# Two reorderings in a fused scan, attention and feed-forward kernel: when the third chunk's norm is issued, and when a group norm's sums follow their transposes

## The chip, the core and the metric

The kernel runs on one core of a Trainium2 chip. A core has five engines that work side by side, each through its own list of instructions: TensorE (PE in the profile, with its weight loads as PEld), VectorE (DVE), ScalarE (ACT), GpSimd (POOL), and SyncE (SP), which issues transfers here. They wait for one another by semaphores. The metric is the device time of one execution in microseconds, the median of several executions. The kernel before takes 1202.92 us (three runs from 1202.42 to 1204.29).

## What is computed

The input is `x` of shape (4, 64, 64, 96) in float32: four images (batches) of 4096 positions with 96 channels. Cut to what matters:

```python
# layer 0
g  = group_norm(x)                          # 32 groups of 3 channels, over a whole image
xn = layer_norm(g) * gamma + beta           # per position, over 96 channels
proj = xn @ W_in + b_in                     # value, gate, delta, and A, B, C (each 96 x 16)
h_t = delta * (A_t * h_{t-1}) + delta * (B_t * value)      # a scan along the 4096 positions
y_t = sigmoid(gate) * sum_s(C_t * h_t)
x  = x + y @ W_out + b_out
# layer 1
t = x as tokens
t = t + linear_attention(layer_norm(t)) @ Wff + bff         # no softmax
t = t + quantized_ffn(layer_norm(t))                        # float8 products, 96 -> 384 -> 96
```

The group norm of an image needs sums over the whole image before its first chunk can be normalised.

## The kernel before

An image is worked in 8 chunks of 512 positions; with 4 images there are 32 chunks, numbered 0 to 31. The scan has 96 x 16 states, which are 12 tiles of 128 rows for each chunk. So there are 384 tiles, and the main loop takes one **step** for each. A chunk is 12 steps; "group 14" below means the 12 steps of chunk 14, and step 168 is its first. The names of the helpers are kept in the text: `b_proj` is three matmuls on TensorE, `b_copy` the ScalarE copy out of PSUM, and so on.

```python
for s in range(min(steps), START): call(s)        # START = 6: whatever is listed for steps below 6
for s in range(START, K):
    tiles[s + 3].b_proj(); tiles[s + 3].b_copy()  # PE; ACT
    tiles[s + 1].a_proj()                         # PE
    tiles[s].c_proj()                             # PE
    tiles[s - 1].keep()                           # ACT: last column of the scan's state
    tiles[s + 2].b_mul()                          # POOL
    if tiles[s - 1].on_pool: tiles[s - 1].c_mul_pool()     # POOL, 4 of 12 tiles
    tiles[s].scan()                               # DVE
    tiles[s + 1].a_mul()                          # DVE
    if not tiles[s].on_pool: tiles[s].c_mul()     # DVE
    call(s)                                       # the other work listed for step s, in order
    if tiles[s].on_pool: tiles[s].c_copy()        # ACT
```

Buffers that matter: PSUM has 1 bank for `b_proj`, 2 for `a_proj`, 1 + 1 for `c_proj` (even and odd tiles), and 3 ("M") for everything else. `b_proj` of the next tile cannot begin before `b_copy` of this one has ended. The order of an engine's instructions is the order in which this program emits them.

The first 54 us or so, with tiles 0 to 5 and the preparation of tiles 6 to 8, come from a list of jobs ordered by hand (`planned_start`). After it, steps from 6 on are emitted by the loop above. All other work is put into `steps` by its offset from the chunk's first step:

```python
AT = {"load_x": -39, "centre": -25, "scale": -24, "stats": -22, "rstd": -22, "apply": -21,
      "transpose": -14, "affine": -13, "upper": -13, "low": -12, ...,
      "gather1": 7, ..., "state_sum": 18, "gated": 18, "project_out": 19, "residual": 19, ...,
      "apply_f": 29, "transpose_f": 30, "quant_in": 31, ..., "sums": -31}

def front(b, i, s0, f=None):          # the norms of chunk i of image b, whose first step is s0
    ...
    plan = [("centre", f.centre, nc.gpsimd), ("scale", f.scale, nc.gpsimd),   # 1 POOL op each
            ("stats", f.stats),                   # DVE: 4 bn_stats, 4 bn_aggr
            ("rstd", f.ln.rstd),                  # POOL: 4 small operations
            ("apply", f.apply), ...]              # ACT: 4 operations
    for name, fn, *args in plan:
        at(s0 + AT[name], fn, *args)
```

Chunks 0 and 1 are normed inside `planned_start`. Chunk 2 (the third) has s0 = 24, so its centre, scale, stats, rstd and apply stand at steps -1, 0, 2, 2 and 3, all below 6, and are emitted between the planned list and step 6.

The group norm of the next image is gathered while this image is worked, one chunk at a time:

```python
def sums(self, n):
    self.transpose(n, "M", "gx")                  # PE: 4 transposes into one M bank
    for k, fn in enumerate((AF.Identity, AF.Square)):          # ACT: two passes with row sums
        nc.scalar.activation(self.ps, self.ps, fn, bias=self.c if k == 0 else 0.0,
                             accum_out=self.s[:, k, n : n + 1])

when = [s0 + AT["sums"] + NT * n for n in range(NCH)]          # NT = 12, NCH = 8
if b == 1: when = [8, 15, 22, 29, 36, 43, 50, 57]
at(when[0] - 2, make)                             # first(): 4 transposes, 2 ACT operations
for n in range(NCH):
    ...
    at(when[n], call, "sums", n)
for n, name in ((1, "moments"), (2, "mean"), (4, "root"), (6, "diagonal"), (8, "spread"),
                (8, "spread_out")):
    at(when[-1] + n, call, name)                  # moments begin with a DVE sum over self.s
```

For images 2 and 3 the sums fall on step 5 of each of the groups 5 to 20; for image 1 on the listed steps of groups 0 to 4. The group norm's entries are listed after those of the chunks, so they come last within a step. The feed-forward part of layer 1 (`apply_f` writes xn, `transpose_f` turns it on TensorE) runs one image behind, from group 10 on, at steps 5 and 6 of a group.

Of the kernel before, what the change touches and what calls it, by code (L numbers as in the profile page):

```python
# [39 lines left out]
AT = {  # L40

    "load_x": -39, "centre": -25, "scale": -24, "stats": -22, "rstd": -22, "apply": -21,
    "transpose": -14, "affine": -13, "upper": -13, "low": -12, "proj_d": -9, "d_out": -9,
    "proj_u": -9, "du_out": -9, "write": -9, "read": -6, "proj_gate": -3, "gate_out": -1,

    "gather1": 7, "gather2": 11, "gather3": 14,

    "state_sum": 18, "gated": 18, "project_out": 19, "residual": 19, "stats_a": 20,
# [5 lines left out]
    "hidden2": 38, "relu2": 38, "project_f": 40, "round_out": 40, "bias_out": 40, "total": 46,  # L54
    "store": 51,

    "sums": -31,
}
ON_POOL = (0, 2, 7, 8)
XBUFS = 15  # L60
# [3 lines left out]
def conv_attn_hybrid_kernel(  # L64
# [462 lines left out]
    def at(step, fn, *args):  # L527
        steps.setdefault(step, []).append((fn, args))
# [4 lines left out]
    class GroupNorm:  # L533
# [34 lines left out]

        def sums(self, n):
            self.transpose(n, "M", "gx")  # L570
            for k, fn in enumerate((AF.Identity, AF.Square)):
                nc.scalar.activation(
                    self.ps, self.ps, fn, bias=self.c if k == 0 else 0.0,
                    accum_out=self.s[:, k, n : n + 1],
                )
# [51 lines left out]
    def group_norm(b, s0):  # L627
        q = {}

        def make():  # L630
            q["g"] = GroupNorm(b)
            q["g"].first()

        def call(name, *args):
            getattr(q["g"], name)(*args)

        when = [s0 + AT["sums"] + NT * n for n in range(NCH)]
        if b == 1:  # L640
            when = [8, 15, 22, 29, 36, 43, 50, 57]
        if b > 1:
            at(when[0] - 7, load_gx, b, 0)
        at(when[0] - 2, make)
        for n in range(NCH):
            if n:
                at(max(when[n] - 7, when[n - 1]), load_gx, b, n)
            at(when[n], call, "sums", n)
        for n, name in ((1, "moments"), (2, "mean"), (4, "root"), (6, "diagonal"), (8, "spread"),
                        (8, "spread_out")):  # L650
            at(when[-1] + n, call, name)
# [107 lines left out]
    def front(b, i, s0, f=None):  # L759
        if f is None:  # L760
            f = Front(b, i)
            plan = [
                ("centre", f.centre, nc.gpsimd), ("scale", f.scale, nc.gpsimd), ("stats", f.stats),
                ("rstd", f.ln.rstd), ("apply", f.apply), ("transpose", f.transpose),
                ("affine", f.affine), ("upper", f.upper), ("low", f.low), ("proj_d", f.proj, 2),
                ("d_out", f.d_out), ("proj_u", f.proj, 0), ("du_out", f.du_out),
                ("write", f.write), ("read", f.read),
            ]
            if (b, i) not in xt:
                plan.insert(0, ("load_x", load_x, b, i))  # L770
        else:
            plan = []
        plan += [("proj_gate", f.proj, 1), ("gate_out", f.gate_out)]
        for name, fn, *args in plan:
            at(s0 + AT[name], fn, *args)

    state = {}
    chs = {}
# [433 lines left out]
    START = 6  # L1212
# [153 lines left out]
    for b in range(B):  # L1366
        for i in range(NCH):
            g = b * NCH + i
            s0 = g * NT
            if g:  # L1370
                front(b, i, s0, second if g == 1 else None)
            for sh in range(1, NSH):
                if g < N - 1 or sh == 1:
                    at(s0 + AT[f"gather{sh}"], gather, g, sh)
            at(s0 + NT, tail, b, i)
            s = s0 + NCH * NT
            first = min(24, AT["fetch"])
            at(s + first if b == B - 1 else min(s + first, K - 4), ffn, b, i, s)
        if b + 1 < B:
            group_norm(b + 1, b * NCH * NT)  # L1380
        s = (b + 1) * NCH * NT
        at(s if s == K else s + AT["gram_add"] - NT + 1, attn_matrix, b, s)
# [82 lines left out]
```

## Time and profile before

| | before |
|---|---|
| median of 3 runs | 1202.92 us |
| span of the profiled run | 1199.1 us |
| TensorE busy | 1148.7 us, 96% (ends of matmuls are modelled) |
| VectorE busy | 1110.0 us, 93% |
| GpSimd busy | 1032.2 us, 86% |
| ScalarE busy | 817.8 us, 68% |
| mean granted TensorE clock | 0.983 |

How the views are read. The windows view gives the busy time of each engine in a stretch, with the number of instructions in brackets, then the granted TensorE clock as a share of full speed, the busy share of the transfer engines and GB/s. The timeline lists, for each run of like instructions, its start and length in us, the engine, the line of the kernel, the operation, output<-input, and in square brackets the idle time of the engine before it and who ended that idle time. The waits view adds those idle times up by pair: us in total, times, longest. Lines of importance: 269 the projections' matmuls, 805 `b_copy`, 808 `b_mul`, 817 `a_mul`, 824 `scan`, 848 `c_mul`, 834 `keep`, 667 and 670 `centre` and `scale`, 371 and 373 `stats`, 378 to 384 and 392 `rstd`, 396 every `apply` on ScalarE, 543 and 572 the transposes and passes of `sums`, 872 `state_sum`, 910 `gated`, 915 and 920 `project_out` and `residual`, 1085 `transpose_f`.

### The profile page before, as it was taken

How to read it: one execution, taken by the hardware profiler on the slowest of the kernel's cores; microseconds unless marked ns; L12 is line 12 of the kernel's file. 1: busy time of each engine (PE TensorE's matmuls, PEld its weight loads, DVE VectorE, ACT ScalarE, POOL GpSimd, SP SyncE). 2: the span in 40 equal slices, each digit the busy share in tenths (PEclk: the TensorE clock that was granted, in tenths of full speed). 3: DMA queues.
4: the chain of work that ended last, by engine and by line, in shares of the span. 5: the costliest groups of instructions: out<-in, count | busy, mean ns of one | idle time of the engine just before them, and what ended most of it. 6: DMA issues, size and time to landing. Idle time of an engine off the chain costs nothing. (4 is left out here: it accounts for less than half of the span.)

```text
span 1199.1 us, 19211 instructions
## 1 busy us (share of the span) xinstructions
PE 1148.7 (96%) x5899; PEld 876.9 (73%) x5899; DVE 1110.0 (93%) x2091; ACT 817.8 (68%) x1828; POOL 1032.2 (86%) x1178
## 2 busy tenths in 40 slices
PE   7799999999999999999999999999999999999885
PEld 6567777677777777777777777777777777777663
DVE  6789999999999999999999999999999999999865
ACT  5465666565555777777777777777777777776476
POOL 3877888888988898999998899999999999988564
PEclk8989999999999999999999999999999999999987
DMA  7566776877776766776677677677776787667221
GB/s 187 127 127 145 153 162 159 175 156 160 168 162 150 162 156 146 175 175 156 155 158 164 152 176 177 135 160 160 163 174 153 163 181 159 151 146 165 60 74 46
DMA packets 104288, 182.12 MB, mean 152 GB/s; under 512 B 42637, under 2 KB 50769, under 8 KB 104186
## 3 DMA queue, kind: packets, MB, share of 16 engines
q1 hardware_dynamic: 90060, 106.96, 37.0%
q0 software_dynamic: 13536, 73.93, 31.0%
q8 instruction: 46, 0.75, 0.3%
q14 instruction: 56, 0.46, 0.1%
q10 hardware_dynamic: 590, 0.02, 0.0%
HBM read 69.12 MB, written 24.77 MB: 78 GB/s over the span
## 5 line engine op out<-in xcount | busy, mean ns | idle before, releaser
L808 POOL TENSOR_TENSOR bu<-bu,rep 128x512 f32<-128x512 f32 x384 | 512.3, 1342 | 53.6 <-ACT state L834 38.5
L824 DVE TENSOR_TENSOR_SCAN h<-Aps,state,bu 128x512 f32<-128x512 f32 x336 | 426.0, 1268 | 0.6 <-POOL ch L857 0.5
L805 ACT ACTIVATE bu<-Bps,b_bac 128x512 f32<-128x512 f32 x384 | 262.3, 683 | 188.7 <-PE Bps L269 185.9
L817 DVE SCALAR_TENSOR_TENSOR Aps<-Aps,b_bac,rep 128x512 f32<-128x512 f32 x384 | 281.8, 734 | 12.6 <-PE Aps L269 12.6
L269 PE MATMUL Bps<-xs,w 128*128 128x512 f32 x768 | 268.5, 431 | 16.1 <-ACT bu L805 15.6
L269 PE MATMUL Aps<-xs,w 128*128 128x512 f32 x768 | 242.4, 396 | 1.2 <-DVE h L824 1.1
L857 POOL TENSOR_TENSOR ch<-ch,h 128x512 f32<-128x512 f32 x128 | 172.5, 1348 | 14.1 <-ACT ch L854 10.7
L269 PEld LDWEIGHTS Aps<-xs,w 128*128 128x128 f32 x768 | 143.6, 188 | 38.0 <-DVE h L824 3.7
L269 PEld LDWEIGHTS Bps<-xs,w 128*128 128x128 f32 x768 | 126.5, 191 | 61.1 <-ACT bu L805 26.3
L269 PE MATMUL Aps<-xl,w 128*128 128x512 f32 x384 | 151.9, 396 | 0.0
L269 PE MATMUL Bps<-xl,w 128*128 128x512 f32 x384 | 151.8, 395 | 0.0
L269 PE MATMUL Dps<-xs,w 128*128 128x512 f32 x384 | 121.0, 396 | 0.0
L269 PE MATMUL Cps<-xs,w 128*128 128x512 f32 x384 | 120.7, 395 | 0.3 <-ACT ch L854 0.3
L848 DVE SCALAR_TENSOR_TENSOR ch<-Dps,b_bac,h 128x512 f32<-128x512 f32 x160 | 118.6, 741 | 0.8 <-PE Dps L269 0.7
L863 POOL DMA_DIRECT2D ch<-ch x94 | 90.1, 958 | 0.8 <-DMA ch<-ch 0.8
L269 PEld LDWEIGHTS Bps<-xl,w 128*128 128x128 f32 x384 | 72.5, 189 | 17.7
L269 PEld LDWEIGHTS Dps<-xs,w 128*128 128x128 f32 x384 | 72.3, 188 | 17.6
L269 PEld LDWEIGHTS Aps<-xl,w 128*128 128x128 f32 x384 | 72.2, 188 | 17.7
L269 PEld LDWEIGHTS Cps<-xs,w 128*128 128x128 f32 x384 | 71.9, 188 | 17.9 <-ACT ch L854 0.4
L854 ACT ACTIVATE ch<-Cps,b_bac 128x512 f32<-128x512 f32 x96 | 65.8, 685 | 22.9 <-PE Cps L269 22.9
L269 PE MATMUL Dps<-xl,w 128*128 128x512 f32 x192 | 75.8, 395 | 0.0
L269 PE MATMUL Cps<-xl,w 128*128 128x512 f32 x192 | 75.7, 394 | 0.0
(200 smaller groups left out, 2048.2 us busy)
## 6 DMA issues: line engine op xcount, KB each, us to landing
ch<-ch POOLq DMA_DIRECT2D x94, 768.0 KB, 6.6
rep<-ddd SPq DMA_DIRECT2D x124, 384.0 KB, 7.0
ddd<-dd SPq DMA_DIRECT2D x31, 384.0 KB, 3.2
xl<-lo SPq DMA_DIRECT2D x62, 128.0 KB, 2.5
x<-in_x_dram SPq DMA_DIRECT2D x32, 192.0 KB, 2.9
xatd<-xat SPq DMA_DIRECT2D x32, 192.0 KB, 3.6
xal<-xatd SPq DMA_DIRECT2D x32, 192.0 KB, 2.9
out_dram<-o SPq DMA_DIRECT2D x32, 192.0 KB, 2.1
```

The costliest lines, as they stand in the source:

```text
L269: nc.tensor.matmul(ps, lhsT=wt[:, n], rhs=mv, start=(n == 0), stop=(n == 2))
L805: nc.scalar.activation(self.bu, self.b_ps, AF.Identity, bias=self.bias(0))
L808: nc.gpsimd.tensor_tensor(self.bu, self.bu, rep[self.b, self.i][:, 1, self.cg], ALU.mult)
L817: nc.vector.scalar_tensor_tensor(self.a_ps, self.a_ps, self.bias(1), rep[self.b, self.i][:, 0, self.cg], ALU.add, ALU.mult,)
L824: nc.vector.tensor_tensor_scan(self.h, self.a_ps, self.bu, 0.0 if self.i == 0 else state[self.sh, self.cg], ALU.mult, ALU.add,)
L848: nc.vector.scalar_tensor_tensor(self.slot(), self.c_ps, self.bias(2), self.h, ALU.add, ALU.mult)
L854: nc.scalar.activation(self.ch, self.c_ps, AF.Identity, bias=self.bias(2))
L857: nc.gpsimd.tensor_tensor(self.ch, self.ch, self.h, ALU.mult)
L863: nc.gpsimd.dma_start(chs[g, 0], chs.pop((g, sh)), accum_op=ALU.add)
```

## The change

Two things move; no instruction is added or removed. First, an entry of `front` that belongs to the norm of the third chunk and would fall before step 6 is put at step 6 (centre and scale), 7 (stats), 8 (rstd) and 9 (apply). No other chunk is affected, because for all later ones these steps are larger. It is meant to let the engines go on with the tiles that the planned list has prepared, rather than pass through the whole norm first. Second, `sums` is split: the four transposes stay where they were, and the two ScalarE passes come one step later, so that ScalarE meets them when TensorE has done its part.

```diff
-    "sums": -31,
+    "sums": -31, "sums_out": -30,
@@
         def sums(self, n):
             self.transpose(n, "M", "gx")
+
+        def sums_out(self, n):
             for k, fn in enumerate((AF.Identity, AF.Square)):
                 nc.scalar.activation(
@@
             at(when[n], call, "sums", n)
+            at(when[n] + AT["sums_out"] - AT["sums"], call, "sums_out", n)
@@
         plan += [("proj_gate", f.proj, 1), ("gate_out", f.gate_out)]
+
+        late = {"centre": 0, "scale": 0, "stats": 1, "rstd": 2, "apply": 3}
         for name, fn, *args in plan:
-            at(s0 + AT[name], fn, *args)
+            step = s0 + AT[name]
+            at(max(step, START + late[name]) if name in late else step, fn, *args)
```

## The prediction

> **What bounds the kernel now.** I read the windows view first. From 100 us to 1150 us TensorE and VectorE are both over 95% busy; TensorE's figure is modelled, so VectorE, which holds 287 to 288 of every 300 us, is the engine whose idle time I count. The one large hole is where the planned list hands over to the loop:
>
> ```profile
> 50.00:60.00 10.00, 4.05 (x19) 2.75 (x17) 6.67 (x16) 1.23 (x3) 8.62 (x11) 0.82 0.78 179
> 60.00:70.00 10.00, 8.37 (x28) 6.67 (x29) 4.98 (x5) 5.80 (x16) 6.74 (x6) 0.67 0.77 150
> ```
>
> The columns after the length are PE, PEld, DVE, ACT, POOL, clock. TensorE works 4.05 of 10 us, then its clock falls to 0.67; VectorE stands at 4.98 of 10. The timeline of that stretch, taken engine by engine, says why:
>
> ```profile
> 54.34 1.03 POOL L667 TENSOR_TENSOR z<-x,gmr 128x384 f32<-128x384 f32 x1
> 55.44 0.99 POOL L670 TENSOR_TENSOR z<-z,gmr 128x384 f32<-128x384 f32 x1
> ...
> 56.47 0.74 DVE L371 BATCH_NORM_STATS2 st_c<-z 128x6 f32<-128x96 f32 x4 [3.33 <-POOL z L670]
> ...
> 59.46 1.54 ACT L396 ACTIVATE z<-z,nmr_c,rstd_c 128x96 f32<-128x96 f32 x4 [8.13 <-POOL nmr_c L384]
> 60.91 0.67 ACT L805 ACTIVATE bu<-Bps,b_bac 128x512 f32<-128x512 f32 x1
> ...
> 61.63 1.22 PE L269 MATMUL Bps<-xs,w 128*128 128x512 f32 x2 [7.44 <-ACT bu L805]
> ```
>
> The norm of chunk 2 crosses GpSimd, VectorE, GpSimd, ScalarE in turn. [...] `b_copy` of tile 9 (its projection was issued at 51.39 and would have been readable at about 52.3) stands behind an apply that begins at 59.46, and TensorE waits 7.44 us for it. Scan 6 begins at 57.40 and scan 12 at 77.16, by the timeline of VectorE.
>
> Next I asked what differs between groups. Counting scan starts in the timeline, group 14 lasts 34.87 us (513.96 to 548.83), group 27 33.49 (961.55 to 995.04), with 33.04 and 32.97 us of VectorE work. The first has the group norm's sums, the second has not. In the stretch from 407 to 724 us, nine groups with sums and feed-forward, the waits view shows:
>
> ```profile
> PEld L1085 <- ACT xn L396: 9.8, 35, 0.3
> DVE yg L910 <- PE y_ps L872: 8.3, 9, 1.4
> DVE x L920 <- PE o_ps L915: 8.1, 9, 1.0
> ```
>
> From 758 to 1062 us, without sums, the first two are absent and the third is 4.7. The timeline of group 14 around step 5:
>
> ```profile
> 530.42 0.65 ACT L572 ACTIVATE gx_ps<-gx_ps,gmc 96x512 f32<-96x512 f32 x1 [1.13 <-PE gx_ps L543]
> ...
> 531.82 1.53 ACT L396 ACTIVATE xn<-x,nmr_f,rstd_f 128x96 fp8e5<-128x96 f32 x4
> 533.25 0.67 ACT L805 ACTIVATE bu<-Bps,b_bac 128x512 f32<-128x512 f32 x1
> ...
> 532.33 1.30 PE L1085 MATMUL xq_ps<-ident,xn 128*128 128x128 fp8e5 x4
> 533.56 1.06 PE L872 MATMUL y_ps<-ch,fold 128*32 128x512 f32 x6
> ...
> 534.71 0.69 DVE L910 TENSOR_TENSOR yg<-y_ps,gate 96x512 f32<-96x512 f32 x1 [0.89 <-PE y_ps L872]
> ```
>
> ScalarE waits 1.13 us for the transposes, spends 1.49 us on the passes (530.42 to 531.91), and only then makes xn. TensorE's four transposes of xn go at the pace of xn (1.30 us; 0.40 us in group 27), state_sum begins late, and VectorE's gated waits 0.89 us.
>
> [...] `b_copy` ran 8.6 us after its data could be read. [...] matmuls of line 269 follow at 0.43 us instead of 0.235 us from 61.63 on, until about 66.5, 4.9 us later. [...]
>
> **The change, part 1: chunk 2's norm.** I carry the engines forward by the durations of this trace, from where they stand at about 54 us.
> - GpSimd, which ends the planned list at 54.4: `b_mul` 8 (1.27) to 55.65, centre (1.03) and scale (0.99) to 57.7, `b_mul` 9 to 58.95, gather (1.07) to 60.0, `b_mul` 10 to 61.3, `c_mul_pool` 7 (1.30) to 62.6, the four rstd operations (57.57 to 59.42 in the trace, 1.85) to 64.4.
> - VectorE: scan 6 begins at 53.1 instead of 57.40; scan 7 at 55.6; stats (1.1) wait until 57.7 for scale; scan 8 at 58.8, 9 at 60.7, 10 at 63.2.
> - ScalarE does `b_copy` 9 at 52.4, 10 at 55.1, 11 at 57.0, 12 at 59.6; TensorE follows without a hole. Then, in step 9, apply waits for rstd until 64.4 and ends at 65.95. In the same step the first sums_out of image 1 comes behind it, 1.49 us, to 67.4; `b_copy` 13 ends at 68.1.
> - TensorE waits for it with the projection of tile 14. `a_proj` 12 is readable 0.7 + 0.7 + 0.16 later, at 69.7. `a_mul` 12 (0.73) and `c_mul` 11 (0.74) put scan 12 at 71.2.
>
> 77.16 − 71.2 = 6.0 us. A second hole remains, in other words, of some 3.5 us on TensorE. Should its clock fall again I lose about 1; half of that taken off, **5.5 us**. Past tile 12 VectorE sets the pace in both kernels, so the shift stays.
>
> **Part 2: the passes.** A group with feed-forward: xn starts right behind `keep`, as in group 27 (943.32, ending before TensorE needs it). Group 27 has xq_ps at 945.95 and state_sum at 946.28, 0.33 later; in group 14 state_sum then starts at 532.33 + 0.33 = 532.66 instead of 533.56, 0.90 earlier. It ends at 533.72, while VectorE is free at about 533.8: the wait of 0.89 is gone. The passes fit into the idle time of ScalarE that follows (2.76 us in group 27). The transposes stay on TensorE, 0.35 us of issue, so the wait for o_ps stays near 0.91 against 0.49 in group 27. So 0.9 us in each of the groups 11 to 20 is 9.0; group 13, whose wait is 1.37, gives 0.45 more, group 10 about 0.3. Groups 5 to 9 have no xn behind the passes and give nothing (groups 6 to 8 already take 31.7 us).
>
> Image 1's sums lie on other steps. Step 15 now has a `b_copy` held 1.4 us by the passes (0.44 us of VectorE idle, which I count as gained), and the first sums of image 2 give about 0.3. At step 51 the passes join d_out (0.68) and apply (1.54): `b_copy` comes 1.6 us later, TensorE is ahead by 0.7, I lose 1.0. At step 58 the moments stand in the step of the last passes: VectorE waits about 0.7. Net −1.0. Part 2: 9.0 + 0.45 + 0.3 − 1.0 = **8.7 us**.
>
> Sum 14.2; 1202.9 − 14.2 = **1188.7 us**.
>
> **The rivals.** (a) *The wait moves.* The same five operations still cross the same engines; only tiles 8 to 11 stand between them. The apply at step 9 could hold ScalarE longer than I reckon, since GpSimd is the fullest engine there (about 16 us of work in 15 us). For it: GpSimd is busy 8.62 of 10 us even with the hole. Against it: it had 6.74 in the next 10. Then part 1 gives 2 to 3, the time is 1191 to 1192. (b) *VectorE alone sets the pace after the hand-over*, rstd being ready earlier: scan 12 at 68.4, 8.8 us gained, 1185. (c) *Part 2 comes to nothing*, because gated then waits for something else, or TensorE, with the transposes still in it, holds state_sum: gain 5.5 less 1.0, about 1198. For it: o_ps still waits. Against: groups 6 to 8 have the same transposes, and no wait for y_ps. (d) *The later passes hold an M bank or a `b_copy`* in many groups: GpSimd's `b_mul` already waits 12.3 us for ScalarE in those nine groups. If each lost 0.5, 16 × 0.5 = 8 less, 1197.
>
> **Range and chances.** Part 1 is 3 to 8, part 2 is 6 to 10 with some doubt whether it arrives at all. That makes 1183.5 to 1195. Two per cent faster is 1178.9 or less, 24 us, which would need both parts to bring nearly twice their sum: 0.04. Slower by 2% would need a new stall of 24 us for which I see no place: 0.02.
>
> **What would show it.** In the profile after: TensorE's idle of 7.44 before line 269 gone and one of about 2 us twice near 64 to 68; scan 12 near 71; clock above 0.9 in 60 to 70; no wait of yg for y_ps, xq_ps back at 0.40, the wait of x for o_ps unchanged; groups 11 to 20 near 33.95 us; a VectorE wait at line 579 in step 58. Wrong I would be if groups 11 to 20 stay at 34.9, or scan 12 does not move by 3 to 8 us.

## The result, and the profile after

| | before | after |
|---|---|---|
| median | 1202.67 us | 1185.72 us |
| lowest to highest, 4 runs each | 1202.33 to 1204.29 | 1184.83 to 1187.49 |
| ratio to before, 95% interval | | 0.9858 [0.9841, 0.9875] |
| span of the profiled run | 1199.1 us | 1185.8 us |
| VectorE busy | 1110.0 us | 1109.0 us |

The changed kernel is 17 us faster; 1188.7 was forecast. The two profiled runs differ by only 13.3 us: that of the kernel before took 1200.8 us, less than its median, and that of the changed kernel, 1187.5, is the longest of its four. VectorE does the same work in less time, so the gain is idle time taken away.

The windows view of the changed kernel at the hand-over (length, PE, PEld, DVE, ACT, POOL, clock, transfer share, GB/s):

```profile
50.00:60.00 10.00, 9.49 (x44) 6.98 (x42) 9.54 (x19) 5.43 (x13) 9.92 (x10) 1.00 0.77 179
60.00:70.00 10.00, 6.05 (x16) 4.40 (x17) 4.39 (x5) 4.10 (x12) 8.46 (x11) 0.66 0.83 167
```

The first ten microseconds, which were half empty, are full. The hole has not gone: it stands ten microseconds later, and the clock falls in it as before (0.66; 0.67 in the kernel before). The timeline of the changed kernel, ScalarE, then TensorE, then VectorE, says what it now waits for:

```profile
64.51 1.54 ACT L396 ACTIVATE z<-z,nmr_c,rstd_c 128x96 f32<-128x96 f32 x4 [4.07 <-POOL nmr_c L384]
...
65.38 0.80 PE L269 MATMUL Dps<-xl,w 128*128 128x512 f32 x1 [3.91 <-DMA w<-w]
...
66.21 0.75 DVE L854 SCALAR_TENSOR_TENSOR ch<-Dps,b_bac,h 128x512 f32<-128x512 f32 x1 [3.57 <-PE Dps L269]
```

ScalarE's apply begins at 64.51, against 64.4 in the forecast. But TensorE is not held by it: in the middle of `c_proj` 9 it waits 3.91 us for the last weight copy, a transfer. SyncE issued that copy at 56.76, behind the four transfers of rep, 384 KB each (from 54.09). Scan 12 begins at 74.03, not at 71.2.

The sums, in the same group 14 (ScalarE, TensorE, VectorE; lines 574, 1091, 878 and 916 are 572, 1085, 872 and 910 of the kernel before):

```profile
522.24 1.54 ACT L396 ACTIVATE xn<-x,nmr_f,rstd_f 128x96 fp8e5<-128x96 f32 x4
524.10 0.69 ACT L811 ACTIVATE bu<-Bps,b_bac 128x512 f32<-128x512 f32 x1 [0.33 <-PE Bps L269]
524.69 0.18 ACT L840 COPY state<-h 128x1 f32<-128x1 f32 x1
524.77 0.65 ACT L574 ACTIVATE gx_ps<-gx_ps,gmc 96x512 f32<-96x512 f32 x1
...
525.31 0.40 PE L1091 MATMUL xq_ps<-ident,xn 128*128 128x128 fp8e5 x4
525.63 1.06 PE L878 MATMUL y_ps<-ch,fold 128*32 128x512 f32 x6
...
526.77 0.69 DVE L916 TENSOR_TENSOR yg<-y_ps,gate 96x512 f32<-96x512 f32 x1
```

xn comes first and the passes fit behind `b_copy`; the transposes of xn take 0.40 us again, and gated has no wait. In the waits view from 403 to 711 us (groups 11 to 19, the nine of the prediction's view) the pair of yg and y_ps has fallen from 8.3 us to 0.6, in two groups alone, and x waits for o_ps as before:

```profile
DVE x L926 <- PE o_ps L921: 7.9, 9, 1.0
DVE yg L916 <- PE y_ps L878: 0.6, 2, 0.4
```

Counting scan starts, group 14 lasts 33.90 us instead of 34.87. Up to scan 12 the profiled run had gained 3.1 us, up to group 5 4.7, and group 5 took 1.5 back; groups 10 to 20, each counted against its own length before, brought 10.15 together.

### The profile page after: what moved, and what is told of

Read it like the earlier page. It is cut to its first block, busy times and chain, and to the rows that moved or that the text cites. A ratio compares the mean times of both kernels' runs of the same rounds, so it can differ in the third digit from the quotient of the medians.

```text
span 1185.8 us, 19197 instructions
## 1 busy us (share of the span) xinstructions
PE 1142.9 (96%) x5899; PEld 876.3 (74%) x5899; DVE 1109.0 (94%) x2091; ACT 818.9 (69%) x1828; POOL 1032.6 (87%) x1178
## 5 line engine op out<-in xcount | busy, mean ns | idle before, releaser
L269 PEld LDWEIGHTS Cps<-xs,w 128*128 128x128 f32 x384 | 72.2, 188 | 18.0 <-ACT ch L860 0.5
L269 PEld LDWEIGHTS Aps<-xl,w 128*128 128x128 f32 x384 | 72.3, 188 | 17.8
L269 PEld LDWEIGHTS Dps<-xs,w 128*128 128x128 f32 x384 | 72.3, 188 | 17.6
```

The source lines that it names most:

```text
L269: nc.tensor.matmul(ps, lhsT=wt[:, n], rhs=mv, start=(n == 0), stop=(n == 2))
```

## Experiments

A word on one sentence ahead of the prediction: it says that the group norm's entries come last within a step. That holds against the norms of later chunks only. Two further parts of a chunk's work, the helpers `tail` and `ffn`, add their entries while the program is being emitted, behind the group norm's; this is why the passes stood in front of xn at all, and in image 1 in front of the attention's apply.

Each ratio below is against the kernel before, run beside it.

### Each part alone

```diff
 # the norm alone
-    "sums": -31, "sums_out": -30,
+    "sums": -31, "sums_out": -31,
 # the sums alone
-            step = s0 + AT[name]
-            at(max(step, START + late[name]) if name in late else step, fn, *args)
+            at(s0 + AT[name], fn, *args)
```

> Part 1 alone: chunk 2's norm behind the planned steps, the passes of the sums where they were before. Theory A (the two parts are independent; the hand-over gained 3.1 us by scan 12 because TensorE then stands 3.9 us before the second half of c_proj 9 for the last weight copy): 2 to 4 us less than before, and a TensorE wait of about 4 us for the copy of w near 61 to 65 us. Rival B (the hand-over is worth the 5.5 us of the prediction and the image 1 sums took some of it back): 5 to 6 us less.

> Part 2 alone: passes one step behind their transposes, chunk 2's norm where it was before. Theory A: groups 10 to 20 shorten by about 0.95 us each as in the changed kernel, some 10 us, and image 1's sums bring between -1 and +2: 9 to 12 us less than before; the 7.44 us hole in front of line 269 stays. Rival B (the gain in the groups needs the shifted hand-over): clearly less than 9.

The norm alone: 1195.89 us (1194.2 to 1201.0) against 1202.49, ratio 0.9952 [0.9935, 0.9969], 5.8 us by the ratio, with an interval from 3.7 to 7.8. TensorE's wait for w is there, 3.0 us in this run. Groups 11 to 20 are as in the kernel before. Here theory A was too low and B's 5.5 us was nearer; the profile of the changed kernel, on which A's figure rested, had caught a long wait. The sums alone: 1191.12 us, ratio 0.9897 [0.9882, 0.9912], 12.4 us with an interval from 10.6 to 14.2, about the upper end of theory A; the hole of 7.45 us in front of line 269 stays. In this trace groups 10 to 20 are as in the changed kernel, so rival B fails. 5.8 and 12.4 make 18.2 against 17: the parts add, within what the intervals leave.

Image 1's sums can be read from the starts of groups in this trace. With the passes a step later, groups 1 and 2 last 1.24 and 1.23 us less, group 3 0.27 less, group 4 1.17 more, group 5 1.58 more.

### What holds the hand-over

The copy or the apply? Two edits, alone and together:

```diff
 # rep's transfers behind the last weight copies (low_c is the last weight's low part)
+        plan.rank = 7
-        job("SP", 1.8, second.read, after=[a])
+        job("SP", 1.8, second.read, after=[a, low_c])
 # rstd a step earlier
-        late = {"centre": 0, "scale": 0, "stats": 1, "rstd": 2, "apply": 3}
+        late = {"centre": 0, "scale": 0, "stats": 1, "rstd": 1, "apply": 3}
```

> The changed kernel, with the four transfers that bring chunk 1's rep issued behind the last two weight copies instead of in front of them. Theory A (the 384 KB of rep hold up the last weight copy): TensorE no longer waits for w; the next hole is the one the prediction reckoned with, apply waiting for rstd until 64.4 and TensorE for b_copy 13 until about 68; scan 12 near 71.2 instead of 74.0; 2 to 3 us less than the changed kernel. Rival B (the copy is held by the 768 KB gather issued at 59.0, or by the gx load at 58.96): the wait for w stays within 0.5 us and so does the time.

> The changed kernel with rstd of chunk 2 at step 7 instead of 8, rep's transfers where the changed kernel has them. Theory A: the weight copy still holds TensorE to 64 or 65 us, so the time stays within 1 us of the changed kernel, though apply is released 2.5 us sooner. Rival B (only the apply counted, the wait for w lay beside it): as much gain as with both, 2 to 4 us.

> The changed kernel, with rep's transfers behind the last weight copies and, besides, rstd of chunk 2 at step 7 instead of 8, so that GpSimd does it before b_mul 10 and c_mul_pool 7. Theory A (two waits lie side by side at the hand-over, the weight copy and apply for rstd; with the copy gone the second alone holds): ScalarE's apply is released near 62 instead of 64.4, TensorE's two holes near 65 and 68 nearly close, scan 12 near 69 instead of 72.0; 2 to 4 us less than with the late read alone. Rival B (GpSimd's total work sets scan 12): scan 12 stays at 71.5 to 72 and the time too.

| rep late | rstd early | scan 12 begins | median | ratio |
|---|---|---|---|---|
| no | no | 74.0 | 1185.72 | 0.9858 [0.9841, 0.9875] |
| yes | no | 72.0 | 1185.72 | 0.9861 [0.9848, 0.9874] |
| no | yes | 73.2 | 1186.08 | 0.9857 [0.9842, 0.9872] |
| yes | yes | 68.7 | 1183.87 | 0.9844 [0.9829, 0.9859] |

With rep late the last weight copy is issued at 54.50 instead of 56.76. TensorE's timeline has no wait for w between 60 and 70, but these two instead:

```profile
64.80 1.39 PE L684 MATMUL xnt_ps<-ident,z 128*96 128x128 f32 x4 [0.56 <-ACT z L396]
67.83 0.73 PE L269 MATMUL Bps<-xs,w 128*128 128x512 f32 x2 [1.64 <-ACT bu L811]
```

These are the forecast's hole: z is ready when apply has ended, and `b_copy` 13 comes behind apply and the passes. With rstd early alone, the copy still holds:

```profile
65.07 0.50 PE L269 MATMUL Dps<-xl,w 128*128 128x512 f32 x1 [3.81 <-DMA w<-w]
```

So two waits lie side by side, and taking away one uncovers the other. The median does not move for either alone, against the 2 to 3 us expected of rep late. Scan 12 of a single trace is a coarse measure: four other kernels here leave the norm and the transfers as the changed kernel has them (the norm alone, and from below the passes behind xn and everything at step 6 and at step 8). In them TensorE waits 2.97, 2.63, 2.95 and 3.89 us for w, and scan 12 begins at 71.6, 72.2, 72.3 and 73.6. The second and third rows of the table lie within that spread; only the fourth stands out. With both waits gone scan 12 begins at 68.7, and at 68.6 and 68.4 in the two kernels under "The best put together", which have both edits too. That is where rival (b) of the prediction put it, 68.4.

Theory A is confirmed for the place, but only part of the time arrives. The median is 1.85 us below that of rep late alone, where 2 to 4 were expected, and the intervals overlap. Group 1 lasts 33.34 us instead of 31.60. The VectorE timeline of that kernel has, in group 1:

```profile
82.86 1.28 DVE L830 TENSOR_TENSOR_SCAN h<-Aps,state,bu 128x512 f32<-128x512 f32 x1 [0.71 <-POOL ch L863]
```

and its waits view from 68.7 to 102 us an apply that waits for GpSimd's nmr, and TensorE's wait for the `b_copy` behind it:

```profile
ACT z L396 <- POOL nmr_c L384: 1.8, 1, 1.8
PE Bps L269 <- ACT bu L811: 1.5, 1, 1.5
```

With rep late alone it is the other way round there: GpSimd waits 1.1 us for VectorE's statistics, apply waits only 0.2 for GpSimd, and TensorE's wait is absent. GpSimd has become what the next norm waits for (it is busy 9.92 of the 10 us from 70 to 80): of the 2.75 us won by scan 12 (the start of scan 0 allowed for), 1.74 are given back twenty microseconds later. Whether rep late takes the wait for w away by the earlier issue of the copy or by the transfers that no longer run beside it was not separated, so rival B of that run is not ruled out.

### Why the passes matter

```diff
 # whole at 6 (or 8): images 2 and 3, transposes and passes in one later step;
# what hangs on `when` (first, moments to spread) moves with them
-            at(when[n] + AT["sums_out"] - AT["sums"], call, "sums_out", n)
+            at(when[n] + (b == 1), call, "sums_out", n)
+        if b > 1:
+            when = [w + 1 for w in when]          # + 3 for step 8
 # behind xn (images 2 and 3): same step 5, but appended while step 5 is emitted
+                at(when[n], at, when[n], call, "sums_out", n)
```

> The changed kernel, but for images 2 and 3 the passes stand in the same step as their transposes, behind xn instead of in front of it. Theory A (the place relative to xn is all that counts): no wait of gated for y_ps, groups 11 to 20 at 33.9 us, the time within 1.5 us of the changed kernel. Rival B (the step between matters, because the passes also hold up b_copy of the same step by 1.2 us): groups at 34.3 or more, 4 us or more above the changed kernel.

1186.23 us, ratio 0.9861 [0.9847, 0.9876], the same as the changed kernel; groups 11 to 20 as there to 0.02 us. ScalarE's timeline in group 14 has xn first and the passes behind it, in one step:

```profile
520.56 1.54 ACT L396 ACTIVATE xn<-x,nmr_f,rstd_f 128x96 fp8e5<-128x96 f32 x4
522.01 0.63 ACT L574 ACTIVATE gx_ps<-gx_ps,gmc 96x512 f32<-96x512 f32 x1
```

The pair of yg and y_ps stands at 0.6 us, as in the changed kernel. Rival B fails: the step between is not needed.

> The changed kernel, but for images 2 and 3 the transposes of the sums move to step 6 as well, so the passes stand in the same step as their transposes again, only not in front of xn. Theory A (what cost 0.9 us a group was that xn, which TensorE needs for the chain to gated, stood behind the passes): groups 11 to 20 stay at 33.9 us and the time within 1.5 us of the changed kernel, though ScalarE again waits about 1 us for the transposes. Rival B (ScalarE's wait for transposes of the same step is the cost): groups 11 to 20 back at 34.9 us, 9 to 10 us more than the changed kernel.

1182.82 us, ratio 0.9837 [0.9824, 0.985]. The waits view from 399.5 to 706.8 us, groups 11 to 19:

```profile
ACT gx_ps L574 <- PE gx_ps L543: 9.6, 9, 1.2
DVE x L928 <- PE o_ps L923: 8.1, 9, 1.1
```

ScalarE waits 1.1 us a group for the transposes again, as in the kernel before, and it costs nothing: group 14 lasts 33.89 us. What cost time was the order, passes before xn, and not the wait within the step. The version is about 3 us faster than the changed kernel, more than theory A allowed, for a reason outside it: the other parts of the group norm move by a step with the sums. Group 5 lasts 33.98 instead of 36.26 us. There the two operations of `first` now come behind a `b_copy` (217.91 behind 217.26) and no longer in front of it (218.95 and 219.79 in the changed kernel); TensorE's wait for that copy is 1.53 us instead of 2.36. Groups 13 and 21, where the next image's mean is spread, take 1.2 and 1.1 less; groups 10 and 17 have 0.4 and 0.5 more. Of these four the cause was not looked for.

> The changed kernel, but for images 2 and 3 the sums (transposes and passes) move to step 8, behind o_ps. Theory A (the remaining 0.42 us of a group is TensorE's 0.35 us of transposes ahead of o_ps): VectorE's wait for o_ps falls from 0.91 to about 0.49, groups 11 to 20 to 33.5 us, 3 to 4 us less than the version with everything at step 6, some 1179 us. Rival B (the transposes cost TensorE time wherever they are): groups stay at 33.9, the time at 1182 to 1183.

1188.35 us, ratio 0.9878 [0.9858, 0.9898]: the median is 2.6 us above the changed kernel's, where both theories had it below, though the intervals overlap. In the traces groups 10 to 20 take 379.0 us against 375.4. The waits view from 404.6 to 714.9 us:

```profile
POOL ch L865 <- ACT ch L862: 14.5, 9, 1.9
ACT gx_ps L574 <- PE gx_ps L543: 9.7, 9, 1.2
...
DVE x L928 <- PE o_ps L923: 5.1, 9, 0.8
```

The wait of x for o_ps falls from 7.9 to 5.1, in group 14 to the expected 0.49, so that step of A is right. But a new wait stands in the first row, absent from the changed kernel's view: at step 8 the passes are in front of `c_copy`, and GpSimd waits 1.6 us a group for it. Group 14 takes 34.26. Neither theory had it.

### The best put together

```diff
 # rep late, rstd early, images 2 and 3 whole at step 6, and for image 1:
+            at(when[n] + (b == 1 and n != 6), call, "sums_out", n)        # first version
+            at(when[n] + (b == 1 and n in (1, 2)), call, "sums_out", n)   # second version
```

> All that helped put together: rep's transfers behind the weight copies, rstd of chunk 2 at step 7, the sums of images 2 and 3 whole at step 6, image 1's passes one step behind their transposes save those of chunk 6, which stay at step 50. If the gains add (about 1.8 from the hand-over, 1.2 from step 50, on top of 1182.8): 1179 to 1181 us, group 4 at 33.9 instead of 35.1. Rival (one is given back elsewhere, as part of the early rstd was in group 1): 1182 or more.

> The same, but of image 1 only the passes of chunks 1 and 2 come a step later; those of chunks 0 and 3 to 7 stand in the step of their transposes. Theory (only chunks 1 and 2 gained by the step between, 1.2 us each, and chunk 6 lost 1.2): within 1 us of the version above. Rival (the others gain too): 1.5 us or more above it.

1179.70 us, ratio 0.9819 [0.9804, 0.9834], and 1177.94 us, ratio 0.9814 [0.9799, 0.9829], against 1201.08. Group 4 takes 33.71 and 33.72 us instead of 35.09, so moving the passes from step 50 to 51 had cost 1.4 us. The two are not told apart: their ranges overlap, and in the traces the last group begins within 0.3 us. Both beat the changed kernel.

## Why the prediction was right, point by point

- **The hole moves rather than closes: right; its cause was wrong.** The forecast gave GpSimd's rstd until 64.4 and apply from then on (64.51 in the trace), scans 6 to 9 at 53.1, 55.6, 58.8 and 60.7 (53.1, 55.6, 58.8, 60.8). The step that failed is "TensorE follows without a hole": its list had no transfer in it. The weight copy needed by `c_proj` 9 held TensorE for 3.91 us, until 65.38, and for 2.6 to 3.9 us in the five kernels with this hand-over. That mis-sized scan 12 (71.2 forecast, 71.6 to 74.0 in these five) but not much the gain: the norm alone brings 5.8 [3.7, 7.8] against 5.5. In part this is luck, for the wait that was left out lay beside the one that was reckoned with and nearly as long. With rep late the forecast's own chain is seen by itself: the two waits of TensorE are 0.56 and 1.64 us, against two of about 2, and scan 12 begins at 72.0. The clock, named as a risk (the half microsecond taken off for it was an estimate), fell in all of these: 0.66 to 0.83 of full speed was granted from 60 to 70 in the five, 0.94 with rep late. With both waits gone it was 1.00.
- **The groups: right within a tenth.** 0.9 us each in groups 11 to 20 was forecast; group 14 gave 0.97. Its wait of yg for y_ps is gone, xq_ps at 0.40, o_ps unchanged at 0.91, its length 33.90 against 33.95. All of groups 10 to 20 brought 10.15 against 9.0 + 0.45 + 0.3. Two single groups were off and nearly cancel: group 10 gave 0.90 instead of 0.3, because its wait for o_ps fell too (0.91 to 0.29), and group 13 gave 0.96 instead of 1.35, because 0.39 us of its wait for y_ps stayed. That the order against xn is the cause is shown by the version with the passes behind xn, and by the one with everything at step 6.
- **Image 1's sums: wrong in sign for some steps.** Forecast −1.0 net; in the trace of the sums alone groups 1 to 5 come to 0.0, and that the errors cancel is luck. Step 15 gave more than the 0.44 counted (group 1 as a whole 1.24), and the 1.23 of group 2 was missed: I did not credit the passes of step 22, which stood in front of the attention's apply and of `b_copy`. Step 51 lost 1.4 (1.0 forecast; group 4 as a whole 1.17). The moments at step 58 do not wait, because the passes come first in that step: they end at 201.90, and VectorE comes to the moments at 202.91. The first sums of image 2 were to give 0.3; group 5 lost 1.5.
- **Group 5 stays partly open.** TensorE's idle before `b_proj` is shorter than before (2.36 us against 2.74), yet from the third on its matmuls then follow one another at 0.42 to 0.43 us, at a granted clock of 0.50 (from 220.4 to 223.4), and in the kernel before at 0.23 to 0.24, at 1.00 (from 225 to 231). First the kernel before, then the changed one:

```profile
225.18 0.73 PE L269 MATMUL Bps<-xs,w 128*128 128x512 f32 x2 [2.74 <-ACT bu L805]
225.75 0.40 PE L269 MATMUL Bps<-xl,w 128*128 128x512 f32 x1
```

```profile
220.51 1.22 PE L269 MATMUL Bps<-xs,w 128*128 128x512 f32 x2 [2.36 <-ACT bu L811]
221.53 0.63 PE L269 MATMUL Bps<-xl,w 128*128 128x512 f32 x1
221.95 1.05 PE L269 MATMUL Aps<-xs,w 128*128 128x512 f32 x2
```

That costs VectorE 2.41 us of waiting for Aps instead of 1.16. Why the clock falls after the shorter gap was not settled. By the pace of the matmuls it fell there in all six profiled kernels whose gap was 2.35 or 2.36 us, in one of them (rep late, rstd early) only 1.3 us after work had resumed; not in the kernel before (2.74) nor in the norm alone (2.78), nor with everything at step 6, where the gap is 1.53. A gap of 1.96 us went both ways: the matmuls fell to 0.43 us each with everything at step 8, and kept their pace in the second version of the best. So the length of this gap alone does not decide it.
- **The rivals.** (a) holds for the place of the hole and, with rstd early, for GpSimd in group 1, but not for its 2 to 3 us, since the norm alone brings 5.8; (b) holds only once both waits are gone; (c) and (d) fail: `b_mul`'s wait for `keep` on ScalarE fell from 12.3 to 6.1 us in the nine groups.
- **The sum.** 14.2 forecast, 17 measured: part 1 5.8 against 5.5, part 2 12.4 [10.6, 14.2] against 8.7. In the trace of the sums alone groups 10 to 20 bring 10.1 instead of 9.75 and groups 1 to 5 0.0 instead of −1.0. That is 1.4 us; the other 2.3 of part 2 lie in no group, and the kernel before was profiled in a run 1.7 us under the median that this part is measured against. The range of the prediction is also a little wider than its parts: 3 to 8 and 6 to 10 make 1184.9 to 1193.9, not 1183.5 to 1195.

## What to carry to other kernels

ScalarE kept to the order of the program here: in the kernel before, `b_copy` 9 ran 8.6 us after its data could be read, behind the norm's apply. On such an engine, ask of each instruction not how long it waits but who stands behind it and what chain hangs on that one: 1.1 us of waiting cost nothing at one place and 0.9 us a group at another. Before a hand-over is forecast by carrying engines forward, put the landing of every transfer issued in the stretch into the list. And where two waits lie side by side, neither can be judged by removing it alone.

## What the hardware showed that was not expected

- A 96 KB weight copy was issued at 56.76 and awaited until about 65.3, some 8.5 us, where the median for these copies over the run is 2.7 us; four transfers of rep of 384 KB each, a 768 KB gather and a load of the next image were issued between 54.09 and 59.00. Which of them held it was not separated.
- After a gap of 2.36 us TensorE's matmuls, from the third on, followed one another at 0.42 to 0.43 us in the changed kernel, at a granted clock of 0.50; after 2.74 us in the kernel before they followed at 0.23 to 0.24, at 1.00. After 1.96 us they slowed to 0.43 with everything at step 8 and kept their pace in the second version of the best.
